# Counting neighbours with 61-row bf16 products ahead of the table lookups in a four-layer graph network

## The chip, the cores and the metric

The kernel runs on one core of one Trainium2 chip. The metric is the device time of one execution, in microseconds; it was measured three times for the kernel before. The trace shows six kinds of work: PE (TensorE matmuls), PEld (TensorE's loads of the stationary operand), DVE (VectorE), ACT (ScalarE), POOL (GpSimd) and the DMA queues. SP and POOL issue most of the DMAs; a DMA that changes the data type is issued by POOL.

## The reference

There are 16 graphs of 1024 nodes with 128 features, and each has a dense 0/1 adjacency matrix. Four layers follow each other; each adds its result to `x` and normalises the rows.

```
x = layernorm(x + L0(x, adj))   # attention over the neighbours
x = layernorm(x + L1(x, adj))   # max over the neighbours
x = layernorm(x + L2(x, adj))   # x plus the sum of the neighbours, then two linear layers
x = layernorm(x + L3(x, adj))   # dilated adjacency, three SAGE layers with batch norms, one linear layer
```

Layer 1 is the one that the change touches:

```
p = x @ (W1 - W2);  q = x @ W2
pre = p[:, :, None, :] + q[:, None, :, :] + b
return max over j of relu(pre[i, j]) * adj[i, j]
```

For every node `i` and feature this is a maximum of `q` over the neighbours `j` of `i`, to which `p + b` is added. Layer 3 first thins the adjacency out ("dilation"), row by row and with each row depending on the rows before it, and then uses what is left three times.

## The kernel before

**Layer 1 as table lookups.** The 1024 possible neighbours are cut into 86 groups of 12 (`PS`), and each group into two sixes (`GS`). For every six, the maximum of `q` over each of its 64 subsets is put into a table (`tables_of`, L482 and L486, on DVE). Which of the 64 subsets is the neighbour set of node `i` in this group is found by a matmul, the *count* (`count`, L814): a stationary matrix `lit` with +1 and -1 is multiplied with rows of the transposed adjacency, and a Relu with the bias `one_less` (1 minus the size of the subset, L815, on ACT) leaves a 1 at the one subset that fits and 0 elsewhere. This one-hot matrix `hot` selects from the table in another matmul, the *lookup* (`look_up`, L845). Since the lookup works in fp32r, the table is split into a `high` and a `low` part, and both are looked up and added in PSUM. The table comes transposed (`table`, L826, cast to `high` by ACT at L829); `low_part` (L834) subtracts `high` from it in the same PSUM bank, and ACT casts the rest to `low` (L836). One table is made for two groups. DVE takes the running maximum `best` over the groups (L910).

**Slots.** One group of one graph is a slot `s`, and there are 16 x 86 = 1376 slots, each with two halves `h` of 512 nodes. The function `slot` writes down the order of the work by hand: within the loop each engine executes its instructions in the order in which `slot` issues them. A half slot issues the lookup of group `s`, then pieces of other layers, then the low part (first half of odd slots), then the count of group `s + 2`, then the table of group `s + 2` (second half of even slots), then the running maximum. The pieces of other layers come from generators: attention of the next graph (`scores`, `attend`), layer 2 and the rest of the graph before (`rest`), the tables of the next graph. Each says by `ask` which engine it needs and for how long, and `advance` lets it go on while that engine has room in this half slot. The dilation (`dilation`) runs through `dilate_on` at its own due times, counted in slots: blocks of 32 rows, each with 31 steps of small POOL instructions (L669 to L679) one after another, after which the hits are written to memory and read back (L686, L689) and used by DVE (`hit_T`, L703) at a slot that is fixed in advance.

**Buffers.** PSUM tiles named `pm` (count) and `pt` (table) share the tag `subset` with two banks, in turn, in the order in which they are issued. The lookup result `pg` has two buffers. SBUF pools rotate in the same way.

**Adjacency.** `load_rows` (L751) brings all rows of a graph as fp8 into `An`, which has three buffers; it is used by the attention (L337) and, a graph later, by layer 2 (L439). `load_columns` (L766) brings 120 rows of the transposed adjacency at a time as fp8 into `AT` (four buffers), for ten groups of counts; two chunks later they are stored by SP into `adj8` in memory (L759). In the tail, layer 3 reads `adj8` back as `near` (`load_near`, L997, by SP).

**Tail.** After the loop, layer 3's three passes run over the 16 graphs; in the first of them the removed edges are taken out of `near` (L1010 to L1016) two graphs ahead.

Of the kernel before, what the change touches and what calls it, by code (L numbers as in the profile page):

```python
# [29 lines left out]
F32 = mybir.dt.float32  # L30
F32R = mybir.dt.float32r
BF = mybir.dt.bfloat16
# [8 lines left out]
P = 128  # L41
# [2 lines left out]
PS = 2 * GS  # L44
PC = 10
CH = PC * PS
NP = -(-N // PS)
TG = 12
R, G = 32, 4
# [12 lines left out]
def subset_tables():  # L62

    half = P // 2
    s = np.arange(half)
    lit = np.zeros((CH, PC, P), np.float32)
    for j in range(CH):
        a, k = divmod(j % PS, GS)
        lit[j, j // PS, a * half:(a + 1) * half] = np.where((s >> k) & 1, 1.0, -1.0)
    size = sum((s >> k) & 1 for k in range(GS))  # L70
    return lit, np.tile(1.0 - size, 2).astype(np.float32).reshape(P, 1)


@with_exitstack
def tile_graph_layers(ctx: ExitStack, tc, a, out):
# [29 lines left out]
    nc.vector.memset(ones_b, 1.0)  # L105
    mhalf = consts.tile([P, T], F32, name="mhalf")
    nc.vector.memset(mhalf, -0.5)
    lit = early.tile([CH, PC, P], F8, name="lit")
    nc.gpsimd.dma_start(out=lit, in_=a["lit"])
    less = early.tile([P, P], F32R, name="less")  # L110
    nc.vector.tensor_scalar_mul(less, ident, -1.0)
    one_less = early.tile([P, 1], F32, name="one_less")
    nc.sync.dma_start(out=one_less, in_=a["one_less"])

    def weight(name, shape=(P, P), how=None, pool=early, queue=nc.scalar):
        t = pool.tile(list(shape), F32, name="w_" + name)
# [77 lines left out]
    x3 = [dram.tile([P, T, D], F32, name=f"x3_{b}") for b in range(B)]  # L194
    removed = dram.tile([K, P, Q, N], BF, name="removed")
    removed_T = dram.tile([K, P, Q, N], BF, name="removed_T")
    adj8 = [dram.tile([N, N], F8, name=f"adj8_{b}") for b in range(B)]


    def transposed(dst, src):  # L200
# [41 lines left out]
    def layers_012():  # L242
# [163 lines left out]
        def rest(b):  # L406
            best = ps.pop(b)
            yield ask("A", 1.06, after=("rest", b - 1) if b else None)
            nc.scalar.activation(best, best, AF.Relu)
            y = w4.tile([P, T, D], F32, name="y1", tag="y")  # L410
            for h in range(2):
                yield ask("PE", 0.44, take=True)
                pt = shared("ph")
                for t in range(4):
                    nc.tensor.transpose(pt[:, t * P:(t + 1) * P],
                                        best[:, (4 * h + t) * P:(4 * h + t + 1) * P], ident)
                yield ask("V", 0.66, give=True)
                nc.vector.tensor_add(y[:, 4 * h:4 * h + 4, :], X[b][:, 4 * h:4 * h + 4, :],
                                     pt.rearrange("p (t d) -> p t d", d=D))
            happened["y1", b] = now  # L420
            yield from norm(X[b], y)
            xT = w4.tile([P, N], F32, name="xT2")
            yield from columns_of(xT, X[b])
            left = w4.tile([P, T, D], F32, name="left", tag="y")
            parts = w4.tile([P, 3, T, D], BF, name="parts")
            for k in range(3):
                yield ask("A", 1.05, delay=2.5 if k else 0.5)
                nc.scalar.copy(parts[:, k], left if k else X[b])
                if k < 2:
                    yield ask("Pool", 0)  # L430
                    nc.gpsimd.tensor_sub(left, left if k else X[b], parts[:, k])
            hT = w4.tile([P, N], F32, name="hT")
            for h, s in enumerate(halves):
                for c in range(T):
                    yield ask("PE", 0.65, take=(c == 0), same=(c > 0))
                    if c == 0:
                        pa = shared("pa")
                    for k in range(3):
                        nc.tensor.matmul(pa, parts[:, k, c, :], An[b][:, c, s], start=(c == 0 and k == 0),  # L439
                                         stop=(c == T - 1 and k == 2))  # L440
                yield ask("V", 0.66, give=True)
                nc.vector.scalar_tensor_tensor(hT[:, s], xT[:, s], eps1, pa, op0=ALU.mult, op1=ALU.add)
            del An[b]
            zT = []
            for k, tag in ((0, "xT2"), (1, "parts")):
                z = w4.tile([P, N], F32, name=f"z{k}", tag=tag)
                yield from product_of(W1[:, k * P:(k + 1) * P], hT, z, AF.Relu, b1[:, k:k + 1])
                zT.append(z)
            y = w4.tile([P, T, D], F32, name="y")
            for h in range(2):  # L450
                q = slice(4 * h, 4 * h + 4)
                for t in range(4):
                    yield ask("PE", 0.5, take=(t == 0), same=(t > 0))
                    if t == 0:
                        py = shared("py").rearrange("p (t d) -> p t d", d=D)
                        nc.tensor.matmul(py, ones_b[:3, :], four(b23), start=True, stop=False)
                    own = slice((4 * h + t) * P, (4 * h + t + 1) * P)
                    for k in range(2):
                        nc.tensor.matmul(py[:, t, :], zT[k][:, own], W2[:, k, :],
                                         start=False, stop=(t == 3 and k == 1))  # L460
                yield ask("V", 0.65, give=True)
                nc.vector.tensor_mul(y[:, q, :], py, nm[:, q, b].unsqueeze(2).to_broadcast([P, 4, D]))
                yield ask("V", 0.65)
                nc.vector.tensor_add(y[:, q, :], y[:, q, :], X[b][:, q, :])
            yield from norm(X[b], y)
            nc.sync.dma_start(out=x3[b], in_=X[b])
            happened["rest", b] = now
# [279 lines left out]
            nc.sync.dma_start(out=X[b], in_=x[b].rearrange("(t p) d -> p t d", p=P))  # L747

        def load_rows(b):
            An[b] = apool.tile([P, T, N], F8, name="An", bufs=3)  # L750
            nc.gpsimd.dma_start(out=An[b], in_=adj[b].rearrange("(t p) m -> p t m", p=P))  # L751

        def load_columns(at):
            b, c = divmod(at, T + 1)
            if at > 1:
                before, k = divmod(at - 2, T + 1)
                rows = min(CH, N - k * CH)
                begin = len(nc.cur_bb.bb.instructions)
                nc.sync.dma_start(out=adj8[before][k * CH:k * CH + rows], in_=AT[at - 2][:rows])  # L759
                behind(nc.cur_bb.bb.instructions[begin - 1], begin)  # L760
            if b < B:
                rows = min(CH, N - c * CH)
                t = AT[at] = apool.tile([CH, N], F8, name="AT", bufs=4)
                if rows < CH:
                    nc.gpsimd.memset(t, 0.0)
                nc.gpsimd.dma_start(out=t[:rows], in_=adjT[b, c * CH:c * CH + rows])  # L766

        An, AT, subs, qs, ps, values, exps, bests, hots, tables = ({} for _ in range(10))
        now, taken, given, held = 0, 0, {}, {}
        pending = {}  # L770
# [35 lines left out]

        def count(s, h):

            b, g = divmod(s, NP)
            c, r = divmod(g, PC)  # L810
            if h == 0:
                hots[s] = w2.tile([P, N], F32R, name="hot", bufs=3)
            pm = psum.tile([P, 512], F32, tag="subset", name="pm", bufs=2)
            nc.tensor.matmul(pm, lit[:, r, :], AT[b * (T + 1) + c][:, halves[h]], start=True, stop=True)  # L814
            nc.scalar.activation(hots[s][:, halves[h]], pm, AF.Relu, bias=one_less)  # L815

        def table(s):

# [20 lines left out]
        def look_up(s, h, pg):  # L839

            at = s % 2
            for k, part in enumerate(tables[s - at]):
                for a in range(2):
                    rows = slice(64 * a, 64 * a + 64)
                    nc.tensor.matmul(pg[:, a], part[rows, at * P:(at + 1) * P], hots[s][rows, halves[h]],  # L845
                                     start=(k == 0), stop=(k == 1))
# [16 lines left out]
        def slot(s, last):  # L863
# [13 lines left out]
            for h in range(2):  # L877
# [3 lines left out]
                if s >= 0:  # L881
                    pg = psum.tile([P, 2, 512], F32, tag="wide", name="pg", bufs=2)
                    look_up(s, h, pg)
                early = s >= 0 and due < now
                if early:
                    dilate_on()
# [1 line left out]
                advance(("A", "V", "Pool"))  # L888
                if s >= 0 and not early:
                    dilate_on()  # L890
                if h == 0 and s % 2 and s + 1 < last:
                    low_part(s + 1)
                if s + 2 < last:
                    count(s + 2, h)
                    if h and s % 2 == 0:
                        table(s + 2)
                if s >= 0:
                    own = bests[b][:, :, halves[h]]
                    if g == 0:
# [12 lines left out]
                hots.pop(s)  # L912

        dilate = dilation()
        due, wants_bank = 0.0, False
        load_x(0)
        for at in range(2):
            load_columns(at)
# [75 lines left out]

    def load_near(b):
        near = ep.tile([P, T, N], F8, name="near", bufs=2)
        nc.sync.dma_start(out=near, in_=adj8[b].rearrange("(c p) i -> p c i", p=P))  # L997
        return near

    def load_gone(b):  # L1000
# [372 lines left out]
```

## Time and profile before

| what | value |
|---|---|
| three runs | 6110.23, 6109.46, 6090.38 us; median 6109.46 us |
| the profiled execution | 6090.76 us, of it span 6089.0 us |
| granted TensorE clock | 0.972 |
| PE busy | 5556.8 us (91% of the span) |
| DVE busy | 4873.7 us (80%) |
| ACT busy | 3992.1 us (66%) |
| POOL busy | 3642.6 us (60%) |
| DMA | 334.28 MB, mean 55 GB/s |

A group of instructions is one line of the program, one engine and one shape: its busy time, the mean of one instruction, the idle time of the engine just before its members and what ended it. Matmuls are pipelined, so the busy time of one matmul contains latency during which the next one already runs; the distance between two starts tells more of PE's pace than a duration. A wait says which engine stood still, at which of its lines, and which instruction of another engine released it.

### The profile page before, as it was taken

The page shows a single profiled execution, that of the slowest core. Times are in us where ns is not written, and L with a number is a line of the kernel's source. Part 1 is how long each engine was busy: PE and PEld are TensorE (multiplying, and loading weights), DVE is VectorE, ACT ScalarE, POOL GpSimd, SP SyncE. Part 2 cuts the span into 40 slices and gives each one's busy share as a digit, 9 for nine tenths or more (in the row PEclk, how much of TensorE's full clock was granted, in tenths as well). Part 3 has the DMA queues.
Part 4 walks back from the last instruction along what each step waited for, and adds up shares of the span by engine and source line. Part 5 has one row for each costly group of instructions (what it writes and reads, how often), then busy time and mean ns, then how long its engine had stood idle before and what let it go on. Part 6 is the DMA issues. An engine that isn't in the chain of part 4 may idle for free.

```text
span 6089.0 us, 93282 instructions
## 1 busy us (share of the span) xinstructions
PE 5556.8 (91%) x30144; PEld 3035.5 (50%) x30250; DVE 4873.7 (80%) x7484; ACT 3992.1 (66%) x7362; POOL 3642.6 (60%) x11879
## 2 busy tenths in 40 slices
PE   5989999999999999999999999999999878999998
PEld 4545454545454545454545454545444435555654
DVE  2888888889889888888888888888889865555455
ACT  3767777777677767677767676767666644444855
POOL 2676767677767767677777777777777641110114
PEclk8999999999999999999999999999999989999999
DMA  6121312121212121212121212121211025554645
GB/s 41 12 35 24 41 26 39 26 41 27 39 26 40 26 38 27 38 27 39 28 38 27 39 26 39 26 38 27 38 27 30 13 54 141 142 143 135 217 164 194
DMA packets 496976, 334.28 MB, mean 55 GB/s; under 512 B 303338, under 2 KB 448228, under 8 KB 492388
## 3 DMA queue, kind: packets, MB, share of 16 engines
q1 hardware_dynamic: 405504, 260.29, 14.6%
q0 software_dynamic: 89008, 67.42, 13.0%
q8 instruction: 237, 3.88, 0.3%
q14 instruction: 255, 2.09, 0.1%
q10 hardware_dynamic: 1972, 0.59, 0.1%
HBM read 362.38 MB, written 133.96 MB: 82 GB/s over the span
## 4 chain that ended last, share of the span: by engine, by line
PE 33%; DVE 11%; ACT 4%; issue 2%; POOL 1%; DMA 1%; SPq 0%; DVEq 0%; ACTq 0%; POOLq 0%
PE pg L845 8%; DVE best L910 5%; PE pagg L1073 5%; PE pm L814 3%; PE po L1103 2%; PE pa L439 1%; PE po L1097 1%; PE pav L397 1%; PE pp L300 1%; ACT hot L815 1%; DVE sub L486 1%; PE prank L599 1%; PE pdeg L1028 1%; DVE near L1016 1%; PE pe L387 1%
## 5 line engine op out<-in xcount | busy, mean ns | idle before, releaser
L910 DVE TENSOR_TENSOR best<-best,pg 128x1024 f32<-128x1024 f32 x2720 | 3260.8, 1215 | 481.2 <-PE pg L845 470.4
L815 ACT ACTIVATE hot<-pm,one_less 128x512 fp32r<-128x512 f32 x2752 | 1889.9, 690 | 728.7 <-PE pm L814 722.6
L845 PE MATMUL pg<-hot,high 64*128 64x512 f32 x5504 | 1400.3, 505 | 204.5 <-DVE best L910 174.6
L845 PE MATMUL pg<-hot,low 64*128 64x512 f32 x5504 | 1109.9, 400 | 0.0
L814 PE MATMUL pm<-AT,lit 120*128 120x512 fp8e4 x2752 | 1079.4, 392 | 4.5 <-ACT low L836 3.5
L845 PEld LDWEIGHTS pg<-hot,high 64*128 64x128 f32 x5504 | 521.2, 186 | 956.1 <-DVE best L910 455.6
L669 POOL TENSOR_SCALAR sc<-low_counts,half_mask,rest 16x1 f32<-16x1 f32 x992 | 361.0, 364 | 395.8 <-DVE rest L655 285.0
L845 PEld LDWEIGHTS pg<-hot,low 64*128 64x128 f32 x5504 | 534.5, 191 | 0.0
L814 PEld LDWEIGHTS <-lit 120*128 120x128 fp8e4 x2752 | 269.1, 98 | 385.5 <-issue 309.3
L674 POOL TENSOR_SCALAR sc<-sc 16x1 f32<-16x1 f32 x992 | 396.4, 400 | 104.9
L836 ACT CAST low<-pt 128x256 fp32r<-128x256 f32 x688 | 256.5, 373 | 254.0 <-PE pt L834 252.8
L671 POOL TENSOR_SCALAR sc<-sc 16x1 f32<-16x1 f32 x992 | 329.1, 332 | 107.4
L1118 POOL TENSOR_TENSOR length<-length,mhalf 128x8 f32<-128x8 f32 x48 | 78.9, 1645 | 486.2 <-DVE length L1117 486.2
L676 POOL TENSOR_SCALAR hit<-V,sc 16x31 bf16<-16x31 bf16 (+30 forms) x992 | 364.5, 367 | 0.0
L677 POOL TENSOR_SCALAR last_rank<-V,sc 16x31 f32<-16x31 bf16 (+30 forms) x992 | 346.9, 350 | 0.0
L834 PE MATMUL pt<-high,less 128*128 128x256 f32 x688 | 277.0, 403 | 67.4 <-ACT high L829 61.5
L486 DVE TENSOR_TENSOR sub<-sub,q 128x24 f32<-128x24 f32 (+11 forms) x768 | 306.8, 401 | 24.7 <-ACT q L304 10.5
L826 PE MATMUL pt<-ident,sub 128*128 128x128 f32 x1376 | 277.0, 283 | 53.2 <-ACT hot L815 51.1
L397 PE MATMUL pav<-v,eT 128*128 128x128 f32 x2048 | 301.5, 292 | 2.0 <-ACT eT L390 2.0
L397 PEld LDWEIGHTS pav<-v,eT 128*128 128x128 f32 x2048 | 255.5, 196 | 73.3 <-issue 55.6
L670 POOL TENSOR_SCALAR sc<-sc 16x1 f32<-16x1 f32 x992 | 239.9, 242 | 86.6
L349 PE MATMUL psc<-kT,qT 128*128 128x256 f32 x1024 | 273.9, 385 | 9.7 <-issue 9.7
(270 smaller groups left out, 9666.2 us busy)
## 6 DMA issues: line engine op xcount, KB each, us to landing
removed<-gone SPq DMA_DIRECT2D x128, 256.0 KB
An<-in_adj_dram POOLq DMA_DIRECT2D x16, 1024.0 KB, 15.0
E<-in_adj_dram POOLq DMA_DIRECT2D x128, 128.0 KB, 6.5
gone_all<-removed POOLq DMA_DIRECT2D x64, 256.0 KB, 10.5
near<-adj SPq DMA_DIRECT2D x16, 1024.0 KB
kept<-near SPq DMA_DIRECT2D x16, 1024.0 KB
share<-share SPq DMA_DIRECT2D x32, 512.0 KB
hidden<-r SPq DMA_DIRECT2D x32, 512.0 KB
```

The costliest lines, as they stand in the source:

```text
L397: nc.tensor.matmul(pav, eT[:, c, :], values[b][:, c, :], start=(c == 0), stop=(c == T - 1))
L486: nc.vector.tensor_max(sub[:, :n_g, n:2 * n], sub[:, :n_g, 0:n], qg[:, 2 * g0:2 * g0 + n_g, k:k + 1].to_broadcast([P, n_g, n]))
L669: gp.tensor_scalar(half, mine, half_mask[:, m], rest[:, n:n + 1], op0=ALU.mult, op1=ALU.add)
L671: gp.tensor_scalar(sf, half, 5.5, sf, op0=ALU.is_gt, op1=ALU.mult)
L674: gp.tensor_scalar(to, at, sf, none, op0=ALU.subtract, op1=ALU.subtract)
L676: gp.tensor_scalar(hit[:, n, n + 1:], V[:, n, n + 1:], at, None, op0=ALU.is_equal)
L677: gp.tensor_scalar(last[:, n + 1:], V[:, n, n + 1:], to, None, op0=ALU.is_le)
L814: nc.tensor.matmul(pm, lit[:, r, :], AT[b * (T + 1) + c][:, halves[h]], start=True, stop=True)
L815: nc.scalar.activation(hots[s][:, halves[h]], pm, AF.Relu, bias=one_less)
L845: nc.tensor.matmul(pg[:, a], part[rows, at * P:(at + 1) * P], hots[s][rows, halves[h]], start=(k == 0), stop=(k == 1))
L910: nc.vector.tensor_max(own, own, pg)
L1073: nc.tensor.matmul(pa[:, s], piece[:, t, :], m[c][:, s], start=(i == 0), stop=(i == 15))
```

## The change

The count of a group contracted over 120 rows of which 12 mattered. Now it contracts over 60 rows plus one.

- `lit` becomes a bf16 tile of 128 partitions in two copies: rows 0 to 59 and 64 to 123 hold the +1 and -1 of five groups each, and rows 60 and 124 hold `one_less`. A new constant `SUB` is 60.
- The column tiles become four fixed bf16 tiles of 128 partitions, set to 1.0 once by DVE. Each chunk of 120 rows is loaded by two DMAs into partitions 0 to 59 and 64 to 123, so that partitions 60 and 124 keep the ones. The bias of L815 goes away: it comes out of the matmul.
- The store to memory is two DMAs as well, in bf16 (`adjb`). `load_near` now has to cast to fp8 and is issued by POOL.
- In the half slot the low part comes directly behind the lookup, ahead of the other work; the table comes ahead of the count; and the count stands directly ahead of the next lookup.
- The lookup takes its two halves of 64 partitions in the order `(1 - counted, counted)`, where `counted` is the half that the last count used.
- `An` has two buffers in place of three, and `rest` loads the rows of its graph a second time, except for the last graph.

```diff
-    lit = early.tile([CH, PC, P], F8, name="lit")
+    lit = early.tile([P, PC // 2, P], BF, name="lit")
     nc.gpsimd.dma_start(out=lit, in_=a["lit"])
+    for part in range(2):
+        nc.gpsimd.dma_start(out=lit[64 * part + SUB:64 * part + SUB + 1],
+                            in_=a["one_less"].rearrange("(o r) m -> o r m", o=1))
...
             yield from norm(X[b], y)
+            if b < B - 1:
+                yield ask("Pool", 0)
+                load_rows(b)
...
-            An[b] = apool.tile([P, T, N], F8, name="An", bufs=3)
+            An[b] = apool.tile([P, T, N], F8, name="An", bufs=2)
...
-                nc.sync.dma_start(out=adj8[before][k * CH:k * CH + rows], in_=AT[at - 2][:rows])
+                for first, n, own in parts_of(k):
+                    nc.sync.dma_start(out=adjb[before][first:first + n], in_=AT[at - 2][own])
...
-                t = AT[at] = apool.tile([CH, N], F8, name="AT", bufs=4)
-                if rows < CH:
-                    nc.gpsimd.memset(t, 0.0)
-                nc.gpsimd.dma_start(out=t[:rows], in_=adjT[b, c * CH:c * CH + rows])
+                t = AT[at] = columns_in[at % len(columns_in)]
+                for first, n, own in parts_of(c):
+                    nc.gpsimd.dma_start(out=t[own], in_=adjT[b, first:first + n])
+        def parts_of(c):
+            for part in range(2):
+                first = c * CH + part * SUB
+                n = min(SUB, N - first)
+                yield first, n, slice(64 * part, 64 * part + n)
+        columns_in = [apool.tile([P, N], BF, name=f"AT{i}") for i in range(4)]
+        for t in columns_in:
+            nc.vector.memset(t, 1.0)
...
-            nc.tensor.matmul(pm, lit[:, r, :], AT[b * (T + 1) + c][:, halves[h]], start=True, stop=True)
-            nc.scalar.activation(hots[s][:, halves[h]], pm, AF.Relu, bias=one_less)
+            part, r = divmod(r, PC // 2)
+            rows = slice(64 * part, 64 * part + SUB + 1)
+            nc.tensor.matmul(pm, lit[rows, r, :], AT[b * (T + 1) + c][rows, halves[h]], start=True, stop=True)
+            nc.scalar.activation(hots[s][:, halves[h]], pm, AF.Relu)
+            counted = part
...
-                for a in range(2):
+                for a in (1 - counted, counted):
...
                     look_up(s, h, pg)
+                if h == 0 and s % 2 and s + 1 < last:
+                    low_part(s + 1)
...
-                if h == 0 and s % 2 and s + 1 < last:
-                    low_part(s + 1)
                 if s + 2 < last:
-                    count(s + 2, h)
                     if h and s % 2 == 0:
                         table(s + 2)
+                    count(s + 2, h)
...
-        nc.sync.dma_start(out=near, in_=adj8[b].rearrange("(c p) i -> p c i", p=P))
+        nc.gpsimd.dma_start(out=near, in_=adjb[b].rearrange("(c p) i -> p c i", p=P))
```

More of the change, by code (lines that the diff above doesn't have):

```diff
@@ L46 @@
 CH = PC * PS
+SUB = CH // 2
 NP = -(-N // PS)
@@ L65, in subset_tables @@
     s = np.arange(half)
-    lit = np.zeros((CH, PC, P), np.float32)
-    for j in range(CH):
+    lit = np.zeros((2, half, PC // 2, P), np.float32)
+    for j in range(SUB):
         a, k = divmod(j % PS, GS)
-        lit[j, j // PS, a * half:(a + 1) * half] = np.where((s >> k) & 1, 1.0, -1.0)
+        lit[:, j, j // PS, a * half:(a + 1) * half] = np.where((s >> k) & 1, 1.0, -1.0)
     size = sum((s >> k) & 1 for k in range(GS))
-    return lit, np.tile(1.0 - size, 2).astype(np.float32).reshape(P, 1)
+    return lit.reshape(P, PC // 2, P), np.tile(1.0 - size, (PC // 2, 2)).astype(np.float32)
 @with_exitstack
@@ L107, in tile_graph_layers @@
     nc.vector.memset(mhalf, -0.5)
-    lit = early.tile([CH, PC, P], F8, name="lit")
+    lit = early.tile([P, PC // 2, P], BF, name="lit")
     nc.gpsimd.dma_start(out=lit, in_=a["lit"])
+    for part in range(2):
+        nc.gpsimd.dma_start(out=lit[64 * part + SUB:64 * part + SUB + 1],
+                            in_=a["one_less"].rearrange("(o r) m -> o r m", o=1))
     less = early.tile([P, P], F32R, name="less")
     nc.vector.tensor_scalar_mul(less, ident, -1.0)
-    one_less = early.tile([P, 1], F32, name="one_less")
-    nc.sync.dma_start(out=one_less, in_=a["one_less"])
     def weight(name, shape=(P, P), how=None, pool=early, queue=nc.scalar):
@@ L196, in tile_graph_layers @@
     removed_T = dram.tile([K, P, Q, N], BF, name="removed_T")
-    adj8 = [dram.tile([N, N], F8, name=f"adj8_{b}") for b in range(B)]
+    adjb = [dram.tile([N, N], BF, name=f"adjb_{b}") for b in range(B)]
     def transposed(dst, src):
@@ L756, in load_columns @@
                 before, k = divmod(at - 2, T + 1)
-                rows = min(CH, N - k * CH)
                 begin = len(nc.cur_bb.bb.instructions)
-                nc.sync.dma_start(out=adj8[before][k * CH:k * CH + rows], in_=AT[at - 2][:rows])
+                for first, n, own in parts_of(k):
+                    nc.sync.dma_start(out=adjb[before][first:first + n], in_=AT[at - 2][own])
                 behind(nc.cur_bb.bb.instructions[begin - 1], begin)
             if b < B:
-                rows = min(CH, N - c * CH)
-                t = AT[at] = apool.tile([CH, N], F8, name="AT", bufs=4)
-                if rows < CH:
-                    nc.gpsimd.memset(t, 0.0)
-                nc.gpsimd.dma_start(out=t[:rows], in_=adjT[b, c * CH:c * CH + rows])
+                t = AT[at] = columns_in[at % len(columns_in)]
[9 more added lines that the diff above has]
+            nc.vector.memset(t, 1.0)
         An, AT, subs, qs, ps, values, exps, bests, hots, tables = ({} for _ in range(10))
@@ L807, in count @@
         def count(s, h):
+            nonlocal counted
             b, g = divmod(s, NP)
@@ L914, in layers_012 @@
         dilate = dilation()
-        due, wants_bank = 0.0, False
+        due, wants_bank, counted = 0.0, False, 0
         load_x(0)
```

## The prediction

> **What bounds the kernel now.** The profiled execution took 6090.76 us (span 6089.0); the median of the runs is 6109.46, 18.7 us more. The page's first part says PE 91% and DVE 80%, but these mix a loop with its tail, so I asked for one stage: the slot loop, from the first to the last running maximum.
>
> ```profile
> core 0: us, PE busy (x) PEld busy (x) DVE busy (x) ACT busy (x) POOL busy (x), PEclk, DMA share, GB/s
> 144.00:4983.00 4839.00, 4461.07 (x24886) 2359.59 (x24991) 4258.74 (x6209) 3363.06 (x6406) 3421.01 (x11469) 0.98 0.21 31
> ```
>
> The loop is 4839 us for 2752 half slots, 1.758 us each. DVE works 1.548 of that (88%). PE's 92% counts matmul latency, so next I read the groups by shape and one half slot of the timeline.
>
> ```profile
> L910 DVE TENSOR_TENSOR best<-best,pg 128x1024 f32<-128x1024 f32 x2720 | 3260.8, 1215 | 481.2 <-PE pg L845 470.4
> L815 ACT ACTIVATE hot<-pm,one_less 128x512 fp32r<-128x512 f32 x2752 | 1889.9, 690 | 728.7 <-PE pm L814 722.6 <-ACT low L836 0.8
> L836 ACT CAST low<-pt 128x256 fp32r<-128x256 f32 x688 | 256.5, 373 | 254.0 <-PE pt L834 252.8
> ```
>
> ```profile
> 3000.92 0.39 PE L814 MATMUL pm<-AT,lit 120*128 120x512 fp8e4 x1
> 3001.24 0.19 PEld L845 LDWEIGHTS pg<-hot,high 64*128 64x128 f32 x2 [0.23 <-issue]
> 3001.24 0.50 PE L845 MATMUL pg<-hot,high 64*128 64x512 f32 x2
> 3001.34 0.19 PEld L845 LDWEIGHTS pg<-hot,low 64*128 64x128 f32 x2
> 3001.57 0.40 PE L845 MATMUL pg<-hot,low 64*128 64x512 f32 x2
> 3001.90 0.11 PEld L590 LDWEIGHTS <-E 128*128 128x128 fp8e4 x2 [0.37 <-issue]
> ```
>
> Starts, not durations, give PE's real pace: count to lookup 0.32 us, high pair to low pair 0.33, low pair to the next 128-row instruction 0.33. Each pair is two 64-row matmuls side by side. A 512-column pass is about 0.215 (L439's matmuls follow each other at that), so about 0.11 is lost behind every lookup, 0.09 to 0.1 ahead of it. Sorted by what lies between two lookups, half slots hold: count alone 548; count and other PE work (0.54 us) 826; those and the low part 416; those and the table 413; count and table 274; count and low part 271. Own work: 0.98, 1.52, 1.76, 1.73, 1.19, 1.20; mean 1.42. So DVE is the larger load, PE follows, and 0.21 us a half slot is lost in their alternation. The waits of the loop say the same:
>
> ```profile
> DVE best L910 <- PE pg L845: 470.4, 839, 8.8
> DVE hit_T L703 <- DMA hit_p<-hit: 26.2, 2, 15.7
> ...
> PEld pg L845 <- DVE best L910: 455.6, 978, 12.1
> ...
> PEld pt L834 <- ACT high L829: 189.3, 300, 2.0
> ...
> PEld pt L826 <- ACT hot L815: 84.3, 104, 16.5
> ```
>
> DVE's 470 us are the prize. Adding its idle time by kind of half slot, 372 of 425 us (gaps over 60 ns) lie where PE has other work, 5 where it has the count alone.
>
> **The Trainium skill.** "TensorEngine Tiling (Array Packing)", Key Properties: changing the tiling mode drains TensorE, while tiles run independently. The trace agrees: 0.11 us behind a lookup. "TensorE: Matmul & The Clock Gate", Part 3, The mechanism: weight loads overlap running matmuls only on other row groups, and matmuls start and end in order. The pairs starting 3 ns apart agree; the order I assume. "ScalarE: Activation LUTs", What ACT_TABLE_LOAD costs: a per-partition pointer operand adds about 93 ns to an ACTIVATE. L815 with its bias takes 690 ns, L332 of the same size without one 598.
>
> **Part by part.** *PE.* A 61-row count occupies one row tile. The lookup's first matmul takes the other, so its weight load (0.107 between L845's loads) hides behind the count. Three passes on the busier tile are 0.645. After other work: drain 0.08, load 0.03, 0.67 to the end of the low pass, 0.78 together, against 0.32 + 0.12 + 0.43 = 0.87 now: 0.09 saved. With nothing between lookups both drains vanish: 0.66 against 0.98, 0.32 saved. Unknown is whether bf16 and fp32r matmuls overlap on two tiles. If not, each count costs 0.215 more than this: gains of 0.09 become losses of 0.12. If better, nothing more, for the busier tile sets it. I take overlap.
>
> *ACT.* 2752 x 0.092 = 253 us less, 7.5% of its load. ACT is not the end's bound; it shortens waits for `high` and `low`, which I value at 25 us.
>
> *Table ahead of the count.* `high` no longer queues behind `hot` (0.69). L826 now takes a bank released a slot ago. I credit 0.16 us of waiting in the 687 table half slots: 110 of the 135 us that L826 waits (84.3 and 51.1). L834's 250 us mostly go, but see next.
>
> *The new wait.* Counts and tables share two banks. Now the second allocation after a table takes the table's bank, whose last reader is `low`, made a half slot earlier. In the old order that was the count one half slot after the low part; in the new one it is the count in the low part's own half slot. Program order has 687 such counts waiting for ACT. From low-part start to `low`'s end takes 0.77 at least, 0.995 in the mean (timeline). With 0.90 (shorter ACT queue) and 0.06 for the semaphore, PE stands 0.66 in the 271 without other work and about 0.2 in the 416 with it: 180 + 83 = 263 us. Behind it stands the lookup of the next half, and DVE behind that. Against it stand the 0.09 and L834's old wait, of which I give 0.30 to each of the 271 and 0.25 to each of the 416 (185 of 250 us): the 271 lose 0.3 each (0.66 - 0.30 - 0.09), the 416 gain 0.15 (0.25 + 0.09 - 0.20).
>
> *What reaches DVE.* A PE saving counts only where PE is behind. Shares chosen from DVE's idle time by kind: 826 x 0.09 x 0.6 = 45; 548 x 0.32 x 0.15 = 26 (there PE waits for the lookup's bank anyway); 416 x 0.15 x 0.7 = 44; 413 x 0.25 x 0.7 = 72; 274 x 0.25 x 0.4 = 27; 271 x -0.3 x 0.6 = -49. Sum 165, with ACT 190 us, 3.9% of the loop.
>
> *What is late next: POOL.* The 31 steps of a dilation block run on POOL at their own pace: about 121 us of a 151 us block, whatever the slots do. From their end, `hit` and `hit_p` need about 5.4 us to land. DVE takes `hit_T` at a fixed slot, from 4.8 to 21 us after that end, so the slack is 5.2 us in the mean, under 3 us in nine of the 32 blocks. Chain start to `hit_T` is 131 us; 3.9% takes 5.1 us of the slack.
>
> ```profile
> L766 POOL DMA_DIRECT2D AT<-in_adjT_dram x144 | 95.2, 661 | 41.1 <-issue 14.1 <-PE pm L814 9.7 <-PE pg L845 7.8
> ```
>
> POOL's issues take more: 288 column loads for 144, at 0.555 (a 64-row one's minimum) 160 us against 95; 15 row reloads at 1.03 add 15; 16 memsets of 0.942 go. Net 65 us, 2 us a block, queued ahead of the steps. Block by block, the excess of 7 us over the slack sums to about 75 us: DVE waits there, PE and all slots behind it. Net in the loop: 190 - 75 = 115.
>
> *Costed at nothing.* Row reloads: ten slots or more ahead of L439, landing in 15.0. SP's 144 extra stores go into a queue that waits more than it issues. Tail: `near`, now cast on POOL, is issued 26 us ahead of first use, where an adjacency load of twice the source bytes lands in 15; POOL stands idle ahead of L1118 for 486.2 us there. Without that cover, 16 x some 5 us. `near` of graph 0 no longer queues behind the weights on SP: -5 to 0. Start: four memsets on DVE, more issues ahead of the first rows: 0 to +5. I take 0 for the two.
>
> Profiled time 6091 - 115 = 5976, median about **5990**.
>
> **Rivals.** (1) *Likeliest*, 5990, own range 5930 to 6060, chance 0.48. (2) *DVE alone binds*: `hit_p` stays in time, PE's saving passes in full. At most 470 us plus; with half of it 6109 - 240 = 5870. For it: DVE's 88%. Against: only two lookup banks, and the slack above. 0.17. (3) *Nothing arrives*: savings fall where PE waits for DVE, `low` eats the rest: 6105. For it: the 548 half slots with the largest saving have 5 us of DVE idle time. 0.15. (4) *Slower, by the new wait*: gains without the low-part half slots are 195 us with ACT's. It decides from 195/687 = 0.28 us of arriving loss in each of these. At 0.45, where an exponential (1.15) or a row negation (1.15) stands ahead of `low` on ACT, 309 us are lost: 6109 + 114 = 6225; at 0.35, 6155. Against: `low` is issued ahead of the half slot's other ACT work. Counts and lookups not overlapping (the change not doing what it says) end here too. 0.20.
>
> **How the numbers follow.** About 0.5%, 31 us, is what this measurement can tell from no change. Faster: all of (2), 0.46 of (1), 0.04 of (3), 0.67. Same: 0.02 and 0.10, 0.12. Slower: 0.01 of (3), (4), 0.21. The range must take in most of (2) and the lower part of (4): 5870 to 6150 leaves out some 0.07 below and 0.12 above.
>
> **What would show it.** In the timeline, high matmuls starting some 0.03 to 0.11 after a count, not 0.32, and a low pair 0.3 to 0.4 later; L815's line near 598 ns; among the waits, PE's count behind ACT `low`, 200 to 300 us in all; `hit_T` behind `hit_p` at 50 to 120 us; DVE idle before its maximum near 300 us; row steps on POOL at their old pace. The prediction is wrong if counts and lookups follow each other at 0.2 us or more, if the wait for `low` passes 400 us, or if POOL's steps prove to be paced by the slots.

## The result, and the profile after

The changed kernel takes 6063.02 us (median; 6060.8 to 6069.12), the kernel before on the same chip 6104.76; the ratio is 0.9937, 95% interval 0.9917 to 0.9957. That is 42 us less, more than the 31 us that can't be told from no change, and about a third of the 119 us forecast.

The first view is the table by stretches: the slot loop, and all that lies behind its last maximum. Columns: stretch, its length, busy time of PE, PE's weight loads, DVE, ACT and POOL (with instruction counts), granted clock, DMA share, GB/s. The changed kernel:

```profile
144.00:4911.00 4767.00, 4385.11 (x24986) 2542.74 (x24984) 4248.16 (x6207) 3189.99 (x6404) 3495.14 (x11606) 0.93 0.26 42
4911.00:6063.00 1152.00, 1032.98 (x4864) 619.18 (x4864) 578.13 (x1147) 579.14 (x874) 205.02 (x362) 0.95 0.56 155
```

The same view of the kernel before, for the stretch behind its loop:

```profile
4983.00:6089.00 1106.00, 1013.26 (x4864) 611.56 (x4864) 578.19 (x1147) 578.02 (x874) 190.74 (x345) 0.97 0.53 161
```

The loop is 72 us shorter, and the tail, which the prediction costed at nothing, 46 us longer with the same work in it. The granted clock in the loop is 0.93, not 0.98. From here on, "loop" is the time from the first to the last DVE operation on the running maximum in a profile (before 4841, after 4770), "tail" what follows (1108 and 1154). Each such figure is of one profiled execution; where two runs have the same loop, it came out 3 to 10 us apart.

Groups of instructions of the changed kernel, which answer to L910, L815 and L766 before:

```profile
L926 DVE TENSOR_TENSOR best<-best,pg 128x1024 f32<-128x1024 f32 x2720 | 3249.9, 1213 | 400.3 <-PE pg L861 384.3
L830 ACT ACTIVATE hot<-pm 128x512 fp32r<-128x512 f32 x2752 | 1639.1, 598 | 681.7 <-PE pm L829 660.1 <-PE pg L861 0.2
L769 POOL DMA_DIRECT2D AT<-in_adjT_dram x288 | 170.9, 595 | 42.4 <-issue 13.8 <-PE pm L829 8.8 <-PE pg L861 5.2
```

`hot` is at 598 ns as worked out, the issues at 595 ns (0.555 was used). DVE's wait for PE ahead of its maximum fell from 470 to 384 us, not to the 300 forecast. One half slot of the timeline (start, duration, engine and operation):

```profile
3002.02 0.39 PE L829 MATMUL pm<-AT,lit 61*128 61x512 bf16 x1
3002.02 0.62 PE L861 MATMUL pg<-hot,high 64*128 64x512 f32 x2
3002.35 0.52 PE L861 MATMUL pg<-hot,low 64*128 64x512 f32 x2
3002.80 0.72 PE L604 MATMUL prank<-steps,ET 128*128 128x512 bf16 x4
```

Count and lookup are recorded as starting together. Over all half slots of that form the median from the count's start to the next 128-row instruction is 0.785 us, before it was 0.975; some 0.1 of that comes back as the drain ahead of the count. A recorded start alone doesn't prove an overlap; the sum does better. A count pass of 0.215 with the lookup behind it at the old spacings (0.335 from high to low, 0.33 from low to the next) would take 0.88. The row tiles do what they were said to do. The waits of the loop, up to 4950 us:

```profile
PEld pg L861 <- DVE best L926: 461.7, 651, 19.2
DVE best L926 <- PE pg L861: 383.1, 646, 10.5
PEld pt L850 <- ACT high L845: 253.4, 548, 10.4
PE pg L861 <- DVE best L926: 223.5, 407, 12.8
PEld pt L842 <- ACT hot L830: 49.0, 103, 0.7
PE pm L829 <- ACT hot L830: 46.6, 41, 18.6
DVE hit_T L708 <- DMA hit_p<-hit: 37.1, 7, 18.2
```

The wait for `low` isn't there: half of the counts behind a low part start before that `low` has ended, a quarter of them 0.48 us before. The two banks do not go strictly in turn, as the part on buffers has it. Every count behind a low part starts at least 0.05 us after the end of the `hot` of the count just before it, so it takes that count's bank, and the count after it takes the table's. The wait is therefore for `hot`: 46.6 us in all, which the kernel before did not have. The low part's wait for `high` stayed (before 189.3, now 253.4 at the weight load and 38 more at the matmul). PE's waits for DVE grew. The tail's waits show one new item: `u` waits 110.2 us (14 times) for the load of `share`, where before it waited 6.7 us, once.

### The profile page after: what moved, and what is told of

It is laid out like the page before. It is cut to its first block, busy times and chain, and to the rows that moved or that the text cites. A ratio compares the mean times of both kernels' runs of the same rounds, so it can differ in the third digit from the quotient of the medians.

```text
span 6063.3 us, 93320 instructions
## 1 busy us (share of the span) xinstructions
PE 5501.1 (91%) x30250; PEld 3226.6 (53%) x30250; DVE 4868.4 (80%) x7488; ACT 3820.6 (63%) x7362; POOL 3735.3 (62%) x12040
## 5 line engine op out<-in xcount | busy, mean ns | idle before, releaser
L830 ACT ACTIVATE hot<-pm 128x512 fp32r<-128x512 f32 x2752 | 1639.1, 598 | 681.7 <-PE pm L829 660.1
L861 PE MATMUL pg<-hot,high 64*128 64x512 f32 x5504 | 1726.9, 558 | 243.6 <-DVE best L926 223.5
L861 PE MATMUL pg<-hot,low 64*128 64x512 f32 x5504 | 1431.3, 415 | 0.0
L829 PE MATMUL pm<-AT,lit 61*128 61x512 bf16 x2752 | 1121.2, 407 | 54.3 <-ACT hot L830 46.7
L861 PEld LDWEIGHTS pg<-hot,high 64*128 64x128 f32 x5504 | 593.7, 198 | 509.1 <-DVE best L926 461.7
L861 PEld LDWEIGHTS pg<-hot,low 64*128 64x128 f32 x5504 | 823.4, 202 | 8.8
L829 PEld LDWEIGHTS <-lit 61*128 61x128 bf16 x2752 | 260.7, 95 | 586.2 <-issue 513.6
L845 ACT CAST high<-pt 128x256 fp32r<-128x256 f32 x688 | 255.8, 372 | 268.1 <-PE pt L842 264.9
L850 PEld LDWEIGHTS pt<-high,less 128*128 128x128 f32 x688 | 134.1, 195 | 321.8 <-ACT high L845 253.8
L842 PE MATMUL pt<-ident,sub 128*128 128x128 f32 x1376 | 295.8, 299 | 1.2 <-ACT hot L830 0.6
## 6 DMA issues: line engine op xcount, KB each, us to landing
near<-adjb POOLq DMA_DIRECT2D x16, 1024.0 KB, 15.4
```

Source lines behind the costliest of these rows:

```text
L829: nc.tensor.matmul(pm, lit[rows, r, :], AT[b * (T + 1) + c][rows, halves[h]], start=True, stop=True)
L830: nc.scalar.activation(hots[s][:, halves[h]], pm, AF.Relu)
L850: nc.tensor.matmul(pt, less, high, start=False, stop=True, skip_group_check=True)
```

## The experiments

Ratios are to the kernel before on the same chip (medians 6094.7 to 6104.8).

**1. The tail: `near` later.**

```diff
 def removals_end(i):      # first_pass; load_near(b + 2) no longer at the pass's top
     if later:
         gones[b + 2] = load_gone(b + 2)
+        nears[b + 2] = load_near(b + 2)
```

> The changed kernel with the load of near of graph b+2 issued directly behind that of gone, some 8 us later in each of the first layer's passes; nothing else differs. Theory: the 2 MB cast load of near is in flight together with the small load of share and makes it land 9.7 us after its issue; moved behind gone it meets nothing that is urgent, share lands in about 6 us, and the 14 passes that issue a near each get back some 2 us: the stretch behind the last maximum falls from 1154 to about 1124 us, the median from 6063 to about 6033. Rival: near comes too late for its own use (issue to landing 15 us, first use 20 us behind the new issue) and PE waits at the removals instead, or share is late from something else: stretch 1145 to 1165, median 6055 to 6075.

Measured: 6032.54 us, ratio 0.9896 (0.9881 to 0.991), tail 1115.5, loop 4775.5. Timeline of one pass, changed kernel: the load of `near`, the load of `share`, and the `u` that needs it.

```profile
5294.62 0.94 POOL L1013 DMA_DIRECT2D near<-adjb  x1 [15.17 <-ACT m L1068]
...
5298.62 0.43 SPq L1061 DMA_DIRECT2D share<-share  x1
...
5309.02 1.29 DVE L1098 TENSOR_TENSOR u<-pagg,share 128x512 f32<-128x512 f32 x2 [7.92 <-DMA share<-share]
```

The kernel before:

```profile
5232.90 0.39 SPq L997 DMA_DIRECT2D near<-adj  x1
...
5237.11 0.43 SPq L1045 DMA_DIRECT2D share<-share  x1
...
5244.65 1.29 DVE L1082 TENSOR_TENSOR u<-pagg,share 128x512 f32<-128x512 f32 x2 [4.99 <-PE pagg L1073]
```

With `near` behind `gone`:

```profile
5284.05 0.38 SPq L1061 DMA_DIRECT2D share<-share  x1
...
5288.69 0.90 POOL L1013 DMA_DIRECT2D near<-adjb  x1 [0.22 <-issue]
...
5291.52 1.29 DVE L1098 TENSOR_TENSOR u<-pagg,share 128x512 f32<-128x512 f32 x2 [4.98 <-PE pagg L1089]
```

In both kernels `near` is issued some 4 us ahead of `share`. Beside the old load `share` is in time (`u` starts 7.5 us behind the issue, held by PE's `pagg`), beside the new one it isn't (10.4 us). Moved, it is in time again, and 39 of the 46 us come back in the tail. `near` itself still arrives for its use (DVE waits 9 us in all for it). The cause is shown. The Trainium skill, "DMA: Bandwidth & Descriptors", SWDGE vs HWDGE vs iDMA, says that software and hardware queues feed the same DMA engines, which take turns between them; these lines agree in so far as `share` beside the larger load is used 10.4 us after its issue, for at most 7.5; the turns themselves no run here shows.

**2. Queue or bytes.**

```diff
 def load_near(b):                                    # kernel before: 1 MB, fp8
-    nc.sync.dma_start(out=near, in_=adj8[b]...)
+    nc.gpsimd.dma_start(out=near, in_=adj8[b]...)
```

> The kernel before with only the queue of near's load changed, from SP to POOL: still 1 MB of fp8 and no cast. If the software queue itself holds up the load of share, the stretch behind the last maximum grows by about 30 us as in the changed kernel, median about 6135. If the doubled bytes with the cast do it, it stays at 1108 us and the median within 10 us of 6105. The loop is untouched, 4837 us in both cases.

Measured: 6094.59 us, ratio 0.9999 (0.9988 to 1.0011), tail 1104.2. So the queue alone costs nothing, although `u` does wait 47.1 us (8 times) for `share` here: its wait for `pagg` shrinks by nearly as much (103.1 to 68.2). It takes the doubled source with its cast. Which of these two was not separated.

**3. The bias alone.** The fp8 count gets a 121st row of ones; tiles for the columns are set to 1 once.

```diff
-    nc.scalar.activation(hots[s][:, halves[h]], pm, AF.Relu, bias=one_less)
+    nc.scalar.activation(hots[s][:, halves[h]], pm, AF.Relu)     # lit, AT: 121 rows
```

> The kernel before with the bias as a 121st row of ones in the fp8 count and no bias pointer; nothing else. hot falls from 690 to 598 ns, 253 us of ACT's loop time. The prediction valued that at 25 us: median about 6080. Rival: ACT is off the path and nothing arrives, 6100 to 6110. Other rival: ACT's copies (hot, high, low) are what PE and so DVE wait for, and 50 us or more arrive, median 6055 or less.

Measured: 6054.49 us, ratio 0.994 (0.9926 to 0.9954), loop 4810.3, tail 1103.6. Alone it brings as much as the whole change.

**4. The order alone.**

```diff
 look_up(s, h, pg)                                    # kernel before, 120-row counts
+low_part(s + 1)      # at h == 0, odd s
 ...
-low_part(s + 1)
 ...
-count(s + 2, h)
 table(s + 2)
+count(s + 2, h)
```

> The kernel before with its order alone changed as in the change: low part directly behind the lookup, table ahead of the count; counts stay 120 rows of fp8 with the bias pointer. The prediction's terms for the order: table half slots 0.16 us each and the low-part half slots without a wait for low, together 70 to 110 us off the loop, median 6000 to 6035. Theory from the two traces: the table's wait for hot falls (135 us to about 50), but the low part now comes some 0.5 us sooner behind the table and its wait for high stays at 250 us or grows; the loop gains 10 to 30 us, median 6075 to 6095. Third: the earlier low part stops PE where it had work to do, and the order alone costs 10 to 40 us.

Measured: 6100.57 us, ratio 1.0016 (1.0008 to 1.0024), loop 4844.3. Its waits, in the loop up to 4900 us:

```profile
PEld pg L845 <- DVE best L910: 561.8, 1037, 12.0
DVE best L910 <- PE pg L845: 466.8, 806, 8.2
PEld pt L834 <- ACT high L829: 233.8, 554, 1.6
...
PE pm L814 <- ACT hot L815: 42.0, 94, 7.5
...
PEld pt L826 <- ACT hot L815: 34.8, 82, 0.7
```

The table's wait for `hot` fell (at the weight load from 66.5 in this stretch to 34.8), and none of it arrived. Part of it came back as the count's wait for `hot`, 42.0 us where there was none; the lookup's wait for DVE took 112 us more (449.6 before), and DVE waits as before (464.0).

**5. Both moves undone, then each.** Three runs on the changed kernel: counts stay 61 rows, the order goes back.

```diff
 # tiles_old_order: both; old_low_place: the first; old_table_place: the second
-low_part(s + 1)      # directly behind look_up
 ...
+low_part(s + 1)      # behind the half slot's other work
-table(s + 2)
 count(s + 2, h)
+table(s + 2)
```

> The changed kernel with both moves of the order undone: low part behind the other work, count ahead of the table; 61-row counts, row of ones and the loads of the change stay. Reference points: the loop (first to last running maximum) 4841 us before, 4770 in the changed kernel, 4810 with the row of ones alone, 4844 with the order alone. If the order is worth nothing in either kernel, the row tiles bring the other 40 us by themselves: loop 4765 to 4785, median 6055 to 6080. If row tiles pay only where a count stands directly ahead of its lookup, as the prediction had it, 687 half slots lose that and the table waits for hot again: loop 4795 to 4830, median 6090 to 6120.

> The changed kernel with the low part again behind the half slot's other work. The prediction's step: an early low part is worth 0.15 us in 416 half slots that arrives, 44 us, so undoing it costs as much: median about 6105. Theory: PE's wait for high (253 us at its weight load and 38 at its matmul) comes from the early place; put back, it falls below 150 us, but the lookup's wait for DVE takes it up: loop 4755 to 4785, median 6050 to 6075.

> The changed kernel with the count again ahead of the table, so that in 687 half slots the table stands between a count and its lookup. The prediction's step: table half slots gain 0.25 us each by the new place, 99 us of it arriving; undone, median about 6160. Theory: PE gains there go into its wait for DVE; 10 to 30 us are lost, loop 4780 to 4800, median 6073 to 6093.

Measured: both old 6131.31 us, ratio 1.0048 (1.0031 to 1.0065), loop 4843.3; low part old 6019.54, ratio 0.9875 (0.9858 to 0.9891), loop 4736.9; table old 6220.35, ratio 1.0203 (1.0185 to 1.0222), loop 4937.6. The first was slower than either case I had expected, the second faster, and the last far beyond what I expected.

Waits up to 4900 us with the low part in its old place:

```profile
DVE best L926 <- PE pg L861: 351.1, 626, 11.6
PEld pt L850 <- ACT high L845: 99.6, 196, 11.2
```

and with the table in its old place, low part early (this loop runs on to 5077):

```profile
DVE best L926 <- PE pg L861: 523.4, 756, 12.2
PEld pt L850 <- ACT high L845: 342.7, 624, 12.0
```

With its matmul's own wait included, an early low part stands at `high` for 168 us more with the table first (291 against 123) and 240 more with the table in its old place (418 against 178), because it was moved closer to the table that makes `high`. The table's place matters with row tiles for a plain reason, seen in start times (unhindered cases, the 25th percentile): from the first of count and table to the lookup takes 0.532 us before, 0.685 with 61-row counts in the old order (count into row tiles, out for the table, in again), and 0.315 with the table first.

With the table first, though, the lookup no longer has the count's pass ahead of it but beside it. So the fair measure runs from the 128-row instruction ahead of the pair to the one behind the lookup: 1.31 us before, 1.56 with row tiles in the old order, 1.21 with the table first. The move saves 0.35 us in each of 687 half slots, some 240 us, of which 106 arrived (4843 to 4737). Of the 0.35, the two further mode changes take 0.25 (1.56 against 1.31, where the counts use all rows): 0.10 ahead of the count and 0.15 between it and the lookup. The other 0.10 (1.31 to 1.21) is what count and lookup gain side by side.

**6. The row of ones, table first, no row tiles.** The order change of the table on experiment 3.

> The kernel before with the row of ones and with the table ahead of the count; low part in its old place, counts of 121 rows. In the changed kernel the table's place is worth 106 us of loop time (4843 against 4737, low part in its old place). Theory: there it is the row tiles' own mode change that the table in between made dear (count into tiles, out of them for the table, into them for the lookup); a count on all rows has no such step to lose, and the table's place is worth 10 to 40 us: loop 4770 to 4800, median 6015 to 6045. Rival, the prediction's reason: the table's wait for hot is what it saves, the same with either count: loop about 4705, median about 5950.

Measured: 6044.21 us, ratio 0.9917 (0.9902 to 0.9931), loop 4799.1. Without row tiles the table's place changes the way to the lookup by 0.003 us (0.529 for 0.532), and it is worth 11 us, little more than the spread of equal loops. Waits up to 4900 us:

```profile
PEld pg L847 <- DVE best L912: 584.3, 1078, 17.4
...
PE pm L816 <- ACT hot L817: 36.6, 29, 16.6
...
PEld pt L828 <- ACT hot L817: 34.0, 84, 0.7
```

PE's wait for `hot` moved rather than fell. Over the loop it was 99 us at the table in experiment 3; here it is 34 there, 22 at the low part and 37 at the count behind the low part, 92 in all. The wait for `high` did fall, from 199 to 87 us, and the lookup's wait for DVE grew by 123.

**7. Which row tile first.**

```diff
-for a in (1 - counted, counted):
+for a in (counted, 1 - counted):
```

> The changed kernel with the order of the lookup's two row tiles turned round: its first matmul is on the tile that the count has just used, so nothing of it can run beside the count; work and results are the same. PE then has about 0.2 us more in each of the 2752 half slots that put count and lookup together, 550 us in all. If PE's time were the bound the loop would grow by that; by the share of DVE's wait that followed PE's saving (71 of some 300 us, a quarter), it grows by 100 to 200 us, median 6160 to 6260. Rival: start times in the trace don't show a real overlap, and nothing changes: median 6055 to 6075.

Measured: 6058.9 us, ratio 0.9944 (0.9926 to 0.9962), loop 4780.1. No difference, so my expectation was wrong. Start times are the same with either order (low products at 0.34 and 0.47 us behind the count, next instruction at 0.785). The records don't name the row tile. The reading that fits both runs is that neither tile holds up the other, and that the busier one sets the time either way.

**8. What PE time is worth, both ways.** Two runs with the low part in its old place: one more pass per half slot, and one less. The second leaves the products with the table's low parts out.

```diff
 # count_twice: the same matmul into the same bank again
 nc.tensor.matmul(pm, lit[rows, r, :], AT[...][rows, halves[h]], start=True, stop=True)
+nc.tensor.matmul(pm, lit[rows, r, :], AT[...][rows, halves[h]], start=True, stop=True)
 # high_pass_only
-for k, part in enumerate(tables[s - at]):
+for k, part in enumerate(tables[s - at][:1]):
```

> The changed kernel with the low part in its old place (loop 4737 us) and each count's matmul issued twice into the same bank: the second gives the same result, PE has one more 61-row pass on the count's row tile, about 0.215 us in each of 2752 half slots, 592 us. It measures what PE time is worth. The prediction let 165 of 401 us of PE saving arrive, 41%: loop about 4980, median about 6260. If DVE is the bound, under 15% arrives: loop under 4825. If PE is, over 70%: loop over 5150. A fuller PE should also be granted the clock of the kernel before again, 0.97 where the changed kernels have 0.935 to 0.94.

> The changed kernel with the low part in its old place (loop 4737 us), and the lookup without its second pass: the products with the low parts of the table are left out, so each half slot has one 64-row pass less on both row tiles, about 0.215 us, 592 us in all; low parts are still made. It is the counterpart of the count issued twice, where 214 of 592 us of added PE time arrived (36%). The prediction's 41% for a saving gives 240 us: loop about 4495, median about 5780. If a saving arrives less than an addition, because PE stands at the lookup banks until DVE has read them, 15 to 25% (the 62 of 396 us that the row tiles brought): loop 4590 to 4650, median 5870 to 5930.

Measured: a pass more 6239.08 us, ratio 1.0236 (1.0218 to 1.0253), loop 4950.5; a pass less 5998.9, ratio 0.9846 (0.9814 to 0.9877), loop 4707.2. Against 4736.9, the 592 us added cost 214 (36%), the 592 us taken away brought 30 (5%), less than either of my two ranges had it. Both loops in the table by stretches, a pass more and then a pass less:

```profile
144.00:5091.00 4947.00, 4729.18 (x27739) 2872.86 (x27738) 4272.15 (x6207) 3213.26 (x6406) 3464.97 (x11607) 0.98 0.25 40
```

```profile
144.00:4847.00 4703.00, 4133.91 (x19374) 2173.40 (x19491) 4221.64 (x6207) 3155.37 (x6405) 3495.14 (x11606) 0.82 0.26 42
```

and the waits with a pass less:

```profile
PEld pg L861 <- DVE best L926: 639.7, 774, 13.8
DVE best L926 <- PE pg L861: 289.1, 456, 11.4
...
DVE hit_T L708 <- DMA hit_p<-hit: 107.0, 23, 13.1
```

Part of what DVE no longer waits for PE (351 to 289) it waits for `hit_T` (50 to 107), PE stands longer at the lookup banks, and PE's granted clock falls to 0.82.

The clock accounts for much of the loss. It is granted in stretches of full and of half speed, so the same half slot (from one maximum's start to the next) can be compared in two runs by the clock it had for more than half of its time. From the run with the low part back to the one with a pass less:

| clock in the two runs | half slots | change, us |
|---|---|---|
| full in both | 1768 | -137 |
| full, then half | 645 | +169 |
| half in both | 325 | -58 |
| half, then full | 13 | -3 |

Where the clock stayed full, 137 us of 380 arrived, 36%. The same sorting gives 48% for the pass more (248 us in 2389 half slots). So most of the gap between 36% and 5% lies in half slots that fell to the half clock. This division is read from the profiles; no run holds the clock fixed.

**9. The best of it.** Low part back, `near` behind `gone`, and at the loop's end `gone` of graph 0 ahead of `near` of graph 1.

```diff
 nears[0] = load_near(0)
 gones[0] = load_gone(0)
+nears[1] = load_near(1)      # was ahead of gones[0]
```

> The changed kernel with what the runs point to: low part back behind the other work, near of graph b+2 issued behind its gone, and at the loop's end gone of graph 0 ahead of near of graph 1. If the two gains lie in different stretches they add: loop 4737 us as with the low part alone, behind it 1115 us less some 3 for the order at the loop's end, median 5985 to 5995. Rival: near of graph 1, now third on the software queue, comes late for its first removals, or the loop's gain depends on what follows it: median 6000 to 6020.

Measured: 5983.57 us, ratio 0.9813 (0.98 to 0.9827), loop 4727.4, tail 1115.5. It is 1.9% faster than the kernel before and 1.3% faster than the changed one.

## Why the prediction was half right

The direction came out, the size didn't: 115 us were forecast between the profiled executions, 26 came. (Between medians it was 119 and 42; the profiled execution before, 6090.76 us, was at the fast end of its kernel.) The loop missed by 44, the tail by 46. The runs make a ladder from before to after, one step each. The predicted column regroups the prediction's own products. Row tiles: 45 and 26, and the 0.09 us inside the other cases, 0.09 x (416 x 0.7 + 413 x 0.7 + 274 x 0.4 + 271 x 0.6) = 77. Table: 0.16 x (413 x 0.7 + 274 x 0.4) = 64. Low part: what is left, 44 - 26 and -49 - 15, is -46.

| step (loop, us) | predicted | measured |
|---|---|---|
| row of ones, ACT | 25 | 31 (4841 to 4810) |
| table ahead of the count, for its waits | 64 | 11 (4810 to 4799) |
| row tiles, with POOL's lateness | 148 - 75 = 73 | 62 (4799 to 4737) |
| early low part | -46 | -33 (4737 to 4770) |
| sum (parts rounded) | 115 | 71 |
| tail | 0 | -46 |

**Failed: "Costed at nothing ... Tail".** I asked whether `near` would be in time for its own use, and it was: 15.4 us from issue to landing. I didn't ask what else is in flight in those 15 us. `share`, a small load behind which PE's next product waits, was. My price "without that cover, 16 x some 5 us" had the wrong victim; 14 passes waited, and moving the load gave 39 us back (experiment 1).

**Failed: "I credit 0.16 us of waiting in the 687 table half slots".** At the table the wait fell, but experiment 6 has 11 us of the loop for it, not 64. Most of the wait for `hot` moved to the low part and to the count behind it, and what was saved at `high` turned into the lookup's wait for DVE. In those half slots PE was not what DVE waited for in the end. With row tiles the move brings 106 us for another reason: without it each table half slot would hold two more mode changes, 0.25 us. From the kernel before to the changed one these half slots win 0.10 us (1.31 to 1.21), which is the prediction's 0.09.

**Failed as a mechanism: "The new wait".** In the changed kernel no count waits for `low`; the bank that the count behind a low part takes is not the table's, as I had derived, but that of the count before it, for whose `hot` it waits 47 us. The early low part costs about what I charged, 33 against 46 us, because it waits for `high`, which I had written off as "L834's 250 us mostly go". I had seen that the low part comes sooner and not that it comes sooner than its own input.

**Left out: the granted clock.** The prediction has no term for it. From the kernel before to the changed one, the 2386 half slots at full clock in both profiles became 128 us shorter, and the 257 that newly lie in stretches of half the clock became 79 us longer (37 the other way 15 us shorter, 71 at half in both 7 us shorter). A term of that size is enough for the 44 us by which the loop missed. It runs through the steps of the ladder, is read from the profiles as in experiment 8, and was not isolated by a run.

**Right: the overlap and ACT.** The sums are those worked out (the 0.09 us comes out, from 1.09 to 0.99 between 128-row instructions around count and lookup), and `hot`'s 92 ns were worth 31 us in the loop (41 between medians) against 25. So 12 to 16% of ACT's saving arrives.

**Right together, each off: row tiles and POOL.** The sum of the two is 62 against 73. But `hit_T` waited only 19 us more in the changed kernel (37.1 and 8.3 for a store, from 26.2), where I charged 75, because the loop won a third of what I assumed; with faster slots the wait grows as I argued (50 us in the best version, 107 with a pass less). Read with `hit_T`'s wait on the ladder's step (26.9 to 50.0), PE's own saving there was some 85, not 148; that division is argued, only the sum is measured. Sorted by clock as in experiment 8, the step is -93 us in 2363 half slots at full clock in both runs, +62 in 262 that fell to half, and -32 in the rest. I had used one share for PE time, 41% on the whole. Experiment 8 shows what it leaves out: 36% of added time arrived, and of time taken away 36% where the clock stayed full, but 5% in all.

**The rivals.** That little arrives (rival 3) is nearest for the loop, for its own reason, PE waiting for DVE's banks. Slower through `low` (rival 4) and DVE alone as the bound (rival 2) did not occur.

## What to carry to other kernels

When a transfer grows, look at what is in flight beside it, not only at its own deadline: here a 2 MB load with a cast, in time itself, made a 0.5 MB load late and ate two thirds of a loop's gain. On row tiles, keep the instructions that use them next to each other; a full-array instruction in between costs two mode changes, and a step moved forward must not overtake what makes its input. On an engine that alternates with another, price saved time well below its size: here less than half of it arrived. Look at the granted clock too: a PE with less to do was granted less of it, and with a pass less that ate most of what the rest had won. Measure with a pass more and a pass less.

## What the runs showed of the hardware

The granted PE clock fell when PE had less to do. In the loop it was 0.98 before, 0.93 with row tiles, 0.82 with a pass less, and 0.98 again with the count twice. In the changed kernel it is cut into stretches of 1.0 and 0.5, in multiples of 3.4 us. In the loop 74 stretches of 0.5 begin. In the 3.4 us ahead of one, PE stands idle for 40% of the time in the mean, against 8% over the loop, but it is seldom idle throughout: only five of PE's gaps are longer than 3.4 us.

The Trainium skill, "TensorE: Matmul & The Clock Gate", The HAM clock gate, says that half rate is the default state and activity releases it. The trace agrees on the half rate: the 128-column bf16 matmuls of L595 and L1028 that follow each other at twice the usual distance (0.107 us for 0.055) all lie inside the 0.5 stretches, 59 of them, and the 1220 at the usual distance all outside. Count and lookup inside such a stretch, and the same time in the table by stretches, with its clock of 0.50:

```profile
2260.74 0.60 PE L829 MATMUL pm<-AT,lit 61*128 61x512 bf16 x1
2260.74 1.03 PE L861 MATMUL pg<-hot,high 64*128 64x512 f32 x2
2261.33 0.86 PE L861 MATMUL pg<-hot,low 64*128 64x512 f32 x2
2262.13 0.93 PE L604 MATMUL prank<-steps,ET 128*128 128x512 bf16 x2
```

```profile
2260.70:2262.20 1.50, 1.50 (x7) 0.81 (x7) 0.98 (x1) 1.13 (x2) 1.16 (x5) 0.50 0.24 31
```

From the count's start to the next 128-row instruction it is 1.39 us there, 0.78 at full clock (medians). This costs loop time. The loops of the changed kernel and of experiment 1 are the same program, but the stretches fell differently: 81 half slots at full clock in the first and half in the second took 1.55 and 1.88 us, and 72 the other way round 1.83 and 1.41.

A 61-row bf16 product and 64-row fp32r products do run at the same time on the two row tiles (0.785 us for count and lookup, where one after the other at the old spacings would take 0.88), and the order in which the tiles' products are issued makes no difference (6058.9 against 6063.0 us). Leaving the row tiles for 128-row work and entering them again cost 0.25 us for the two changes (1.56 against 1.31).
